# Moving parts of the scan's and of the deformable layer's elementwise work between VectorE, GpSimd and TensorE

## The chip, the cores and the metric

The kernel runs on one core of one Trainium2 chip. The metric is the time of one execution on the device, in microseconds (us); less is better. The engines are named as in the profile: PE is TensorE's matmul and PEld its weight load, DVE is VectorE, ACT is ScalarE, POOL is GpSimd, SP is SyncE, which issues most DMAs.

## The reference, cut to what matters

Four images of 128 channels and 128 x 128 positions, fp32, go through four layers, each `x = x + layer(group_norm(x))`.

- Layer 0 is a deformable 3 x 3 convolution. For each of the 9 taps and each position, a convolution gives an offset and a mask. The input is sampled at the offset place, bilinearly: `corner(y0, x0) + corner(y0, x0+1) + corner(y0+1, x0) + corner(y0+1, x0+1)`, each corner multiplied by its weight and the mask. Then the sampled values are multiplied by the tap's 128 x 128 weight.
- Layer 1 is a dilated convolution, layer 3 a 3 x 3 convolution with a difference term.
- Layer 2 has a selective scan: 128 channels, 16 states, four directions of 16,384 steps, for each image:

```
delta = softplus(dts + dt_b)
dA = exp(delta * A)                      # one per channel and state
h = h * dA + (delta * u) * b             # per channel and state; b per state
y = sum over the states of h * c
```

Before and after the scan stand projections, small convolutions, norms and a gate.

## The kernel before, in words

**Scan.** The positions of one image and direction are cut into 32 blocks of 512 (N); over four images and four directions that is `seq`, 512 blocks. A block has four groups g (NG = 4). A group holds 32 channels times four of their states on the 128 partitions, and has four tiles of 512 along the free axis, called states below (ng = 0 to 3); so 16 scans of 128 x 512 make up a block. For one group the engines do the following:

- SP spreads `delta` and `du = delta * u` from DRAM over the partitions (`spread`, L872); `bb` and `cb`, the b and c of the reference, are spread once for a block (L885).
- ACT copies `du` into a PSUM bank (`inputs_up`, L879). The bank carries the tag `dub`, of which there is one; `prepare` uses the same one for two projections.
- DVE forms the input of all four states in one product of 128 x 2048, `h = du * bb` (L972).
- ACT forms the decays, `exp(delta * A)`, in PSUM (`decay`, L899).
- DVE runs four scans in place (L1018). ACT copies the last column to `carry` (`carry_on`, L933).
- The product `h * cb` is done on two states at a time (`outputs`, L939, 128 x 1024), half 0 and half 1 of a group. It is POOL's. Beside the deformable layer half 1 is DVE's (`on_vector`). Beside layers that load PE, POOL also adds the last two states of each second group (L941), so that PE has one matmul less.
- PE sums over states and partitions with the matrix `gather` into `yacc` (`sums`, L913).

The tiles `h` have five buffers. `prepare(t + 2)` makes delta, du, b and c two blocks ahead. It is a generator: each `next(more, None)` in the scan's loop runs it up to its next `yield`, one slot at a time, 15 in a block. Softplus is `relu(v) + ln(1 + e) + (e - ((1 + e) - 1))` with `e = exp(-|v|)`: ACT computes the functions, POOL the two sums and the difference (L858, L860, L862), and then `du` (L864).

**Deformable layer.** For every block of 512 positions and tap (index n, 1152 in all, 288 for each image) `gather` reads, by four indirect DMAs from POOL's queue (L424), the four corners of each of 4 x 128 positions into the tile `g` of four buffers. ACT multiplies three corners by their weights (`weigh_low`, L438), the first into a PSUM bank `pw`. DVE adds the second and the third to it (`weigh`, L450, two instructions of 128 x 512) and then the fourth with its weight (L453, four of 128 x 128, into `v`). PE transposes `v` (`turn`, L461), ACT copies it out (`copy`, L465), PE multiplies by the tap's weights (`project`, L471). `weave` interleaves these steps: each has a delay in iterations, and stands in one of five places of an iteration. The delays are 0 for gather, 2 for weighing, 3 for turn and copy, 4 for project.

**Order.** The work on every engine is in program order (`keep_order`). The scan of image b runs beside the other layers of its neighbours: `together` lets a generator of the other layers advance with the scan's progress. `loads` writes into `beside["busy"]` which engine the layer at hand loads most: "POOL" beside the deformable layer, "PE" beside layers 1, 2 and 3 of most images, None otherwise. The first image's layers 0 and 1 have no scan to run beside. The order does not depend on any time, so the same instructions stand beside each other in every execution.

Of the kernel before, what the change touches and what calls it, by code (L numbers as in the profile page):

```python
# [10 lines left out]
F32 = mybir.dt.float32  # L11
# [3 lines left out]
ALU = mybir.AluOpType  # L15
# [3 lines left out]
P = 128  # L19
# [4 lines left out]
N = R * W  # L24
# [7 lines left out]
NG = 4  # L32
# [79 lines left out]
def conv_preact_kernel(ctx: ExitStack, tc: tile.TileContext, a: dict, nb: int):  # L112
    nc = tc.nc
    x_in, out = a["x"], a["out"]

    const = ctx.enter_context(tc.tile_pool(name="const", bufs=1))
    small = ctx.enter_context(tc.tile_pool(name="small", bufs=2))
    dram = ctx.enter_context(tc.tile_pool(name="dram", bufs=2, space=DRAM))
    pss = ctx.enter_context(tc.tile_pool(name="scps", bufs=1, space=PSUM))
# [11 lines left out]
    beside = {}  # L131
# [19 lines left out]

    ident = const.tile([P, P], F32, name="ident")
    make_identity(nc, ident)
    started = len(tc.nc.cur_bb.bb.instructions)
    nc.scalar.preload_act_table_set(LOG_EXP)
    gmat = load(const, a["gmat"], [P, P], "gmat_sb")
# [23 lines left out]
    with ExitStack() as s:  # L180
# [3 lines left out]
        for k in range(NDIR):  # L184
            pw = bank(0, "pwd")
# [112 lines left out]
    def layer0(st):  # L298
# [5 lines left out]
        with ExitStack() as s:  # L304
# [139 lines left out]

            def weigh(n):
                i, k, j, q = where(n)
                wv, g = got["i", j][0], got.pop(("g", n))
                pw = got.pop(("w", n)).rearrange("p (r c) -> p r c", r=R)
                for c in (1, 2):
                    nc.vector.tensor_add(pw, pw, g[:, :, c, :])  # L450
                got["v", n] = v = gp.tile([P, R, P], F32, name="v", bufs=2)
                for r in range(R):
                    nc.vector.scalar_tensor_tensor(  # L453
                        v[:, r, :], g[:, r, 3, :], wv[:, r, q, k, 3:4], pw[:, r, :], ALU.mult, ALU.add
                    )

            def turn(n):
                v = got.pop(("v", n))
                got["t", n] = pst = bank(1, "pst")
                for r in range(R):  # L460
                    nc.tensor.transpose(pst[:, r * P : (r + 1) * P], v[:, r, :], ident)  # L461

            def copy(n):
                got["c", n] = smp = pp.tile([P, N], F32, name="smp")
# [322 lines left out]
    def scan(pull):  # L787
# [14 lines left out]
        def decays(at):  # L802

            beside["decays"] = lambda: decays(at + 1)
            while ahead["made"] < min(at + 2, len(seq) * NST):
                decay(ahead["made"])
                ahead["made"] += 1
# [11 lines left out]
                    flush()  # L819
                blocks[t]["u"] = load(sp, blk(us[k % 2], i), [P, N], "u", bufs=2)  # L820

        def prepare(t):

            st, k, i, back = seq[t]
            c = blocks[t]
            if (st["b"], k) not in carries:
                carries[st["b"], k] = carry = small.tile([P, NST], F32, name="carry")
                nc.vector.memset(carry, 0.0)
            c["carry"] = carries[st["b"], k]
            u = c["u"]  # L830
            pdt = pss.tile([P, N], F32, name="pdt", tag="dub")
            nc.tensor.matmul(pdt, wd[:, k, :], u, start=True, stop=True)  # L832
            yield

            dtb = col(V_DTB + k)
            e = sp.tile([P, N], F32, name="e", bufs=1)
            nc.scalar.activation(e, pdt, AF.Abs, bias=dtb)  # L837
            steps = sp.tile([P, 2, N], F32, name="steps")
            delta, du = steps[:, 0, :], steps[:, 1, :]
            nc.scalar.activation(delta, pdt, AF.Relu, bias=dtb)  # L840
            yield
            nc.scalar.activation(e, e, AF.Exp, scale=-1.0)
            yield
            one_e = sp.tile([P, N], F32, name="one_e", bufs=1)
            nc.scalar.activation(one_e, e, AF.Identity, bias=1.0)
            yield
            px = pss.tile([P, N], F32, name="pxbc", tag="dub")
            nc.tensor.matmul(px, xbc[:, k, :], u, start=True, stop=True)  # L848
            ln = sp.tile([P, N], F32, name="ln", bufs=1)
            nc.scalar.activation(ln, one_e, AF.Ln)  # L850
            yield
            nc.scalar.activation(one_e, one_e, AF.Identity, bias=minus)  # L852
            bc = sp.tile([2 * NST, N], F32, name="bc")
            nc.scalar.copy(bc, px[0 : 2 * NST])  # L854
            c["bc"] = bcd = dram.tile([2, NST, N], F32, name="bcd", bufs=4)
            store(bcd.rearrange("j s t -> (j s) t"), bc)
            yield
            nc.gpsimd.tensor_sub(e, e, one_e)  # L858
            yield
            nc.gpsimd.tensor_add(ln, ln, e)  # L860
            yield
            nc.gpsimd.tensor_add(delta, delta, ln)  # L862
            yield
            nc.gpsimd.tensor_mul(du, delta, u)  # L864
            c["steps"] = sd = dram.tile([P, 2 * N], F32, name="stepsd", bufs=4)
            store(sd, steps.rearrange("p j t -> p (j t)"))
# [9 lines left out]
        def inputs_up(t, g):  # L876

            blocks[t]["pdu", g] = p = pss.tile([P, N], F32, name="dub", tag="dub")
            nc.scalar.copy(p, blocks[t]["p", g][:, 1, :])  # L879

        def spread_states(t, what):

# [52 lines left out]
        def outputs(t, g, half, engine=nc.gpsimd):  # L935

            c = blocks[t]
            h = c["h", g][:, 2 * half : 2 * half + 2, :]
            engine.tensor_mul(h, h, c["cb"][:, 2 * half : 2 * half + 2, :])  # L939
            if half and g % 2 and beside.get("busy") == "PE":  # L940
                engine.tensor_add(h[:, 0, :], h[:, 0, :], h[:, 1, :])  # L941
                c["added", g] = True
# [17 lines left out]
        for t, (st, k, i, back) in enumerate(seq):  # L960
            c = blocks[t]
            carry = c["carry"]
            more = prepare(t + 2) if t + 2 < len(seq) else iter(())
            if t > 0:
                fetch(t + 3)
            for g in range(NG):
                then = (t, g + 1) if g + 1 < NG else (t + 1, 0)
                soon = (t, g + 2) if g + 2 < NG else (t + 1, g + 2 - NG)
                before = (t, g - 1) if g else (t - 1, NG - 1)
                earlier = (t, g - 2) if g > 1 else (t - 1, g + NG - 2)  # L970
                c["h", g] = h = hp.tile([P, NG, N], F32, name="h")
                nc.vector.tensor_tensor(  # L972
                    h, c["pdu", g].unsqueeze(1).to_broadcast([P, NG, N]), c["bb"], ALU.mult
                )
                on_vector = beside.get("busy") == "POOL"
                if before[0] >= 0:
                    carry_on(*before, 1)
                if soon[0] < len(seq):
                    spread_steps(*soon)
                at = t * NST + g * NG  # L980
                decays(at)
                if g == 1:
                    if t + 1 < len(seq):
                        spread_states(t + 1, "bb")
                if g == 2 and t + 1 < len(seq):
                    spread_states(t + 1, "cb")
                if g == 3 and back:
                    c["before"] = load(sp, blk(st["y"][k % 2], i), [P, N], "before", bufs=1)
                for ng in range(NG):
                    n = g * NG + ng  # L990
                    if ng == 1:
                        decays(at + 1)
                        if before[0] >= 0 and not on_vector:
                            outputs(*before, 1)
                        if g > 1 and then[0] < len(seq):
                            inputs_up(*then)
                        if earlier[0] >= 0:
                            sums(*earlier, 1)
                    if ng == 2 and g == 1 and t > 0:
                        finish(t - 1)  # L1000
                    if n % NST and ng != 2:
                        next(more, None)
                    if ng == 2 and before[0] >= 0 and on_vector:
                        outputs(*before, 1, nc.vector)
                    if ng == 2:
                        carry_on(t, g, 0)
                        decays(at + 2)
                        next(more, None)
                        if g < 2:
                            inputs_up(*then)  # L1010
                    if ng == 3:
                        outputs(t, g, 0)
                        if before[0] >= 0:
                            sums(*before, 0)
                    o, f = h[:, ng, :], c["a", n]
                    if back:
                        o, f = o[:, ::-1], f[:, ::-1]
                    nc.vector.tensor_tensor_scan(o, f, o, carry[:, n : n + 1], ALU.mult, ALU.add)  # L1018
                    if ng == 3:
                        decays(at + 3)  # L1020
                    yield (t * NST + n + 1) / slots
            for _ in more:
                pass
# [409 lines left out]
```

## Time and profile before

| | us |
|---|---|
| median of three runs | 22,396.11 (22,355.13 to 22,411.09) |
| the profiled execution's own time | 21,942.39 |
| its span, first to last instruction | 21,940.6 |
| PE, PEld busy | 16,289.2 (74%), 6635.1 (30%) |
| DVE busy | 18,903.6 (86%) |
| ACT busy | 16,411.9 (75%) |
| POOL busy | 17,213.1 (78%) |
| mean granted TensorE clock | 0.874 |

Busy time says how long an engine had an instruction under way; its share of the span is an average over stages that have different limits. A row of the groups of instructions has the line, engine and operation, the names out<-in, shapes and count, then the busy time and the mean in ns, and then the engine's idle time before these instructions with what ended it. A fp32 matmul appears as two records, a transpose as one.

### The profile page before, as it was taken

Reading aid. Unit: us, or ns where it says so; the run is one execution under the profiler, and the core shown is the slowest. Engines: PE = TensorE matmul, PEld = TensorE weight load, DVE = VectorE, ACT = ScalarE, POOL = GpSimd, SP = SyncE. Lnnn points to the kernel's source line nnn. Section 1 sums busy time; section 2 is a strip of 40 time slices with the busy share of each in tenths; the row PEclk is TensorE's granted clock in tenths of the full one; section 3 lists DMA queues with packets and bytes.
Section 4 is the critical chain, followed back from the end, with each engine's and each line's share of the span. In section 5 each row is a group of like instructions: output and inputs, shape, how many; then the busy total and the mean of one; then the engine's idle time right before and its main releaser. Section 6 shows DMA issues by size and latency. Waiting matters only on the chain. (4 is left out here: it accounts for less than half of the span.)

```text
span 21940.6 us, 177438 instructions
## 1 busy us (share of the span) xinstructions
PE 16289.2 (74%) x37000; PEld 6635.1 (30%) x37000; DVE 18903.6 (86%) x19821; ACT 16411.9 (75%) x37350; POOL 17213.1 (78%) x11496
## 2 busy tenths in 40 slices
PE   4557866666788878666688888766687878778788
PEld 1223322222333333222233333322233323233333
DVE  4554899999998899899998899998998899999994
ACT  5885868888688766788868776688877877666673
POOL 4773878877888888778788888787878889877884
PEclk6668988888999989888899999887898999999999
DMA  8775687777766968777776787777776677555674
GB/s 250 229 226 178 210 287 243 243 237 237 235 215 216 256 224 272 233 250 249 241 231 220 221 254 249 245 246 245 246 256 210 219 217 233 194 195 202 208 233 132
DMA packets 2578828, 5038.92 MB, mean 230 GB/s; under 512 B 1060736, under 2 KB 1333576, under 8 KB 2435408
## 3 DMA queue, kind: packets, MB, share of 16 engines
q1 hardware_dynamic: 2209104, 3819.31, 53.3%
q0 software_dynamic: 368640, 1208.25, 18.1%
q14 instruction: 782, 6.41, 0.1%
q8 instruction: 302, 4.95, 0.1%
HBM read 4082.03 MB, written 874.52 MB: 226 GB/s over the span
## 5 line engine op out<-in xcount | busy, mean ns | idle before, releaser
L1018 DVE TENSOR_TENSOR_SCAN h<-pa,carry,h 128x512 f32<-128x512 f32 x8192 | 9998.0, 1267 | 495.7 <-ACT pa L899 283.6
L913 PE MATMUL yacc<-h,gather_sb 128*128 128x512 f32 x15264 | 8338.4, 676 | 1770.5 <-POOL h L939 1170.3
L939 POOL TENSOR_TENSOR h<-h,cb 128x1024 f32<-128x1024 f32 x3740 | 8787.1, 2363 | 1093.0 <-ACT carry L933 1076.8
L424 POOL DMA_INDIRECT g<-table,idx x4608 | 4552.7, 988 | 1616.0 <-issue 1059.3
L899 ACT ACTIVATE pa<-spread,neg_a 128x512 f32<-128x512 f32 x8192 | 5488.2, 682 | 271.7 <-DVE h L1018 270.8
L972 DVE TENSOR_TENSOR h<-dub,bb 128x2048 f32<-128x2048 f32 x2048 | 4659.9, 2275 | 418.9 <-ACT dub L879 162.9
L913 PEld LDWEIGHTS yacc<-h,gather_sb 128*128 128x128 f32 x15264 | 3133.5, 216 | 6082.3 <-issue 3392.2
L461 PE MATMUL pst<-ident,v 128*128 128x128 f32 x4608 | 1194.5, 371 | 2578.5 <-DVE v L453 2236.1
L438 ACT ACTIVATE g<-g,wt 128x128 f32<-128x128 f32 x9216 | 2877.5, 389 | 301.5 <-DMA g<-table,idx 298.5
L933 ACT COPY carry<-h 128x2 f32<-128x2 f32 x4096 | 769.0, 188 | 3035.9 <-DVE h L1018 3031.8
L450 DVE TENSOR_TENSOR pw<-pw,g 128x512 f32<-128x512 f32 x2304 | 1597.7, 693 | 1073.6 <-ACT pw L438 1022.6
L438 ACT ACTIVATE pw<-g,wt 128x128 f32<-128x128 f32 x4608 | 1693.6, 368 | 291.2 <-DVE v L453 177.4
L461 PEld LDWEIGHTS pst<-ident,v 128*128 128x128 f32 x4608 | 718.5, 158 | 3938.6 <-issue 1901.5
L858 POOL TENSOR_TENSOR e<-e,one_e 128x512 f32<-128x512 f32 x512 | 651.2, 1272 | 1294.8 <-ACT one_e L852 1258.2
L471 PE MATMUL acc<-smp,w_sb 128*128 128x512 f32 x2304 | 1550.9, 762 | 56.1 <-DVE x L478 52.8
L879 ACT COPY dub<-spread 128x512 f32<-128x512 f32 x2048 | 1198.7, 585 | 391.2 <-DVE h L972 212.7
L453 DVE SCALAR_TENSOR_TENSOR v<-g,wt,pw 128x128 f32<-128x128 f32 x4608 | 1292.8, 342 | 113.7 <-DVE pw L450 2.8
L1238 PE MATMUL p<-xn,w_l_sb 128*128 128x508 f32 (+2 forms) x2304 | 1132.9, 610 | 1.8 <-ACT xn L1217 1.8
L848 PE MATMUL pxbc<-u,xbc_sb 128*128 128x512 f32 x1024 | 590.5, 660 | 394.4 <-DVE h L972 385.9
L721 PE MATMUL px<-win,convw_sb 128*128 128x508 f32 (+1 forms) x1536 | 786.8, 610 | 36.1 <-DMA win<-win 34.8
L941 POOL TENSOR_TENSOR h<-h 128x512 f32<-128x512 f32 x558 | 710.8, 1274 | 43.7
L832 PE MATMUL pdt<-u,wd 128*128 128x512 f32 x1024 | 562.4, 632 | 193.3 <-DVE h L972 127.4
(170 smaller groups left out, 16751.3 us busy)
## 6 DMA issues: line engine op xcount, KB each, us to landing
spread<-stepsd SPq DMA_DIRECT2D x2048, 512.0 KB, 4.3
bb<-bcd SPq DMA_DIRECT2D x512, 1024.0 KB, 8.0
cb<-bcd SPq DMA_DIRECT2D x512, 1024.0 KB, 9.1
stepsd<-steps SPq DMA_DIRECT2D x512, 512.0 KB, 3.5
table<-gt SPq DMA_DIRECT2D x512, 256.0 KB, 4.8
g<-table,idx POOLq DMA_INDIRECT x4608, 3.8
u<-urow SPq DMA_DIRECT2D x256, 256.0 KB, 3.5
yrow<-y SPq DMA_DIRECT2D x256, 256.0 KB, 9.3
```

The source lines that it names most:

```text
L424: nc.gpsimd.indirect_dma_start(out=g[:, r].rearrange("p q c -> p (q c)"), out_offset=None, in_=table, in_offset=bass.IndirectOffsetOnAxis( ...
L438: nc.scalar.activation(pw[:, r * P : (r + 1) * P] if c == 0 else g[:, r, c, :], g[:, r, c, :], AF.Copy, scale=wv[:, r, q, k, c : c + 1],)
L450: nc.vector.tensor_add(pw, pw, g[:, :, c, :])
L453: nc.vector.scalar_tensor_tensor(v[:, r, :], g[:, r, 3, :], wv[:, r, q, k, 3:4], pw[:, r, :], ALU.mult, ALU.add)
L461: nc.tensor.transpose(pst[:, r * P : (r + 1) * P], v[:, r, :], ident)
L471: nc.tensor.matmul(got["a", i], w0[:, k, :], got.pop(("c", n)), start=k == 0, stop=k == KK - 1)
L879: nc.scalar.copy(p, blocks[t]["p", g][:, 1, :])
L899: nc.scalar.activation(pa, blocks[t]["p", g][:, 0, :], AF.Exp, scale=neg_a[:, k, n : n + 1])
L913: nc.tensor.matmul(c["y"], gather[:, g, :], c["h", g][:, ng, :], start=g == 0 and ng == 0, stop=last and ng == parts[-1] and not second,)
L939: engine.tensor_mul(h, h, c["cb"][:, 2 * half : 2 * half + 2, :])
L972: nc.vector.tensor_tensor(h, c["pdu", g].unsqueeze(1).to_broadcast([P, NG, N]), c["bb"], ALU.mult)
L1018: nc.vector.tensor_tensor_scan(o, f, o, carry[:, n : n + 1], ALU.mult, ALU.add)
```

## The change

- A constant `less`, the negative of the identity matrix, is made at the start.
- **Fourth neighbour.** `weigh` no longer adds the third corner (index 2, already weighted by ACT). `turn` instead adds it on PE: for each of the four rows, one matmul of `g[:, r, 2, :]` with the identity and one of `v[:, r, :]` with the identity accumulate into the same part of the bank. They take the place of one transpose. The tile `g` is released after `turn`, not after `weigh`.
- **Softplus's sums.** If the block starts beside the deformable layer (`on_pe`), `prepare` skips two slots, sums `e`, minus `one_e`, `ln` and `delta` by four matmuls into the bank `dub`, and copies the sum to `delta` on ACT one slot later. `du` follows in slot 11 where it was slot 10. `inputs_up` for groups 2 and 3 then stands at ng = 2, where that for groups 0 and 1 already is.
- **Half 0 of the last group.** Beside the deformable layer, half 0 of group 3 goes to DVE as well.
- **Fourth state's input.** Where the deformable layer is not beside the scan, POOL forms the input of the last state of every second group (`last_input`, called at ng = 2 of groups 1 and 3 for the group after), straight from `spread`. DVE's product L972 then covers three states.

```diff
@@ constants
     make_identity(nc, ident)
+    less = const.tile([P, P], F32, name="less")
+    nc.vector.tensor_scalar_mul(less, ident, -1.0)
@@ weigh(n)
-                wv, g = got["i", j][0], got.pop(("g", n))
+                wv, g = got["i", j][0], got["g", n]
                 pw = got.pop(("w", n)).rearrange("p (r c) -> p r c", r=R)
-                for c in (1, 2):
-                    nc.vector.tensor_add(pw, pw, g[:, :, c, :])
+                nc.vector.tensor_add(pw, pw, g[:, :, 1, :])
@@ turn(n)
-                v = got.pop(("v", n))
+                v, g = got.pop(("v", n)), got.pop(("g", n))
                 got["t", n] = pst = bank(1, "pst")
                 for r in range(R):
-                    nc.tensor.transpose(pst[:, r * P : (r + 1) * P], v[:, r, :], ident)
+                    dst = pst[:, r * P : (r + 1) * P]
+                    nc.tensor.matmul(dst, g[:, r, 2, :], ident, start=True, stop=False)
+                    nc.tensor.matmul(dst, v[:, r, :], ident, start=False, stop=True)
@@ prepare(t, on_pe=False)
-            nc.gpsimd.tensor_sub(e, e, one_e)
-            yield
-            nc.gpsimd.tensor_add(ln, ln, e)
-            yield
-            nc.gpsimd.tensor_add(delta, delta, ln)
-            yield
+            if on_pe:
+                yield
+                yield
+                pd = pss.tile([P, N], F32, name="psum", tag="dub")
+                for n, (t, sign) in enumerate(((e, ident), (one_e, less), (ln, ident), (delta, ident))):
+                    nc.tensor.matmul(pd, sign, t, start=n == 0, stop=n == 3)
+                yield
+                nc.scalar.copy(delta, pd)
+                yield
+            else:
+                nc.gpsimd.tensor_sub(e, e, one_e)
+                yield
+                nc.gpsimd.tensor_add(ln, ln, e)
+                yield
+                nc.gpsimd.tensor_add(delta, delta, ln)
+                yield
             nc.gpsimd.tensor_mul(du, delta, u)
@@ new function
+        def last_input(t, g):
+            c = blocks[t]
+            c["h", g] = h = hp.tile([P, NG, N], F32, name="h")
+            nc.gpsimd.tensor_mul(h[:, NG - 1, :], c["p", g][:, 1, :], c["bb"][:, NG - 1, :])
@@ the scan's loop
-            more = prepare(t + 2) if t + 2 < len(seq) else iter(())
+            on_pe = beside.get("busy") == "POOL"
+            more = prepare(t + 2, on_pe) if t + 2 < len(seq) else iter(())
...
-                c["h", g] = h = hp.tile([P, NG, N], F32, name="h")
+                ready = ("h", g) in c
+                if not ready:
+                    c["h", g] = hp.tile([P, NG, N], F32, name="h")
+                h, n = c["h", g], NG - 1 if ready else NG
                 nc.vector.tensor_tensor(
-                    h, c["pdu", g].unsqueeze(1).to_broadcast([P, NG, N]), c["bb"], ALU.mult
+                    h[:, 0:n, :], c["pdu", g].unsqueeze(1).to_broadcast([P, n, N]), c["bb"][:, 0:n, :], ALU.mult
                 )
...
-                        if g > 1 and then[0] < len(seq):
+                        if g > 1 and then[0] < len(seq) and not on_pe:
                             inputs_up(*then)
...
+                        if g % 2 and not on_vector and then[0] < len(seq):
+                            last_input(*then)
                         next(more, None)
-                        if g < 2:
+                        if (g < 2 or on_pe) and then[0] < len(seq):
                             inputs_up(*then)
                     if ng == 3:
-                        outputs(t, g, 0)
+                        outputs(t, g, 0, nc.vector if on_vector and g == NG - 1 else nc.gpsimd)
```

More of the change, by code (lines that the diff above doesn't have):

```diff
@@ L820, in fetch, with prepare @@
                 blocks[t]["u"] = load(sp, blk(us[k % 2], i), [P, N], "u", bufs=2)
-        def prepare(t):
+        def prepare(t, on_pe=False):
             st, k, i, back = seq[t]
```

## The prediction

> **What bounds the kernel now.** I read the busy time by stretch first, because the page's averages mix stages: 0 to 1650 us is the first image's deformable layer alone; three stretches (3250-5350, 8850-10850, 14120-16080, together 6060 us) are the scan beside the next image's deformable layer ("deformable stage" below); the other 13,400 us or so, from 2000 on, are the scan beside other layers ("scan stages"). Columns: stretch, its length, then busy us (and instructions) of PE, PEld, DVE, ACT, POOL, the granted clock of TensorE, DMA share, GB/s.
>
> ```profile
> 9000.00:10500.00 1500.00, 988.45 (x2577) 409.52 (x2578) 1361.49 (x2119) 1328.29 (x3687) 1203.42 (x1067) 0.81 0.77 247
> 6000.00:8500.00 2500.00, 2016.89 (x4285) 820.27 (x4284) 2293.59 (x1724) 1860.16 (x3567) 2134.86 (x1180) 0.93 0.73 233
> 19000.00:20500.00 1500.00, 1182.96 (x2556) 482.92 (x2555) 1449.04 (x1048) 925.55 (x1858) 1200.16 (x611) 0.95 0.57 197
> 500.00:1500.00 1000.00, 578.57 (x1580) 217.93 (x1580) 580.46 (x1418) 864.86 (x2606) 756.78 (x799) 0.67 0.76 228
> 18000.00:18500.00 500.00, 409.70 (x825) 160.12 (x824) 471.49 (x343) 387.39 (x763) 464.90 (x262) 0.95 0.77 237
> ```
>
> In the scan stages DVE is the bound: 97% at 19000, 92% at 6000. POOL follows at 80 and 85%, and at 18000 (four POOL products per block of the output stage) it has 93%.
>
> The deformable stage seems to have three near-equal engines: DVE 91%, ACT 89%, POOL 80%. The groups of lines of 9000 to 10500 (busy, mean ns, then idle before and its releasers) settle it:
>
> ```profile
> L424 POOL DMA_INDIRECT g<-table,idx x899 | 892.4, 993 | 269.4 <-issue 216.7 <-ACT pw L438 21.1 <-DMA g<-table,idx 5.0
> ...
> L450 DVE TENSOR_TENSOR pw<-pw,g 128x512 f32<-128x512 f32 x450 | 311.4, 692 | 103.4 <-ACT pw L438 95.1 <-DMA g<-table,idx 0.4
> ...
> L461 PE MATMUL pst<-ident,v 128*128 128x128 f32 x900 | 223.1, 359 | 500.7 <-DVE v L453 420.2 <-ACT g L438 28.5 <-ACT smp L465 19.5
> L939 POOL TENSOR_TENSOR h<-h,cb 128x1024 f32<-128x1024 f32 x84 | 199.4, 2374 | 9.1 <-ACT carry L933 8.2
> ```
>
> The 269 us before the gathers are mostly "issue", some 0.3 us between one gather and the next. With them POOL is at 1203 + 269 + about 25 = 1497 of 1500 us: POOL is the bound here, at 1.25 us a gather. The lone stage confirms it: 400 gathers in 500 us, 1.25 each, four per neighbour point, 5.0 us a point.
>
> **What the Trainium skill says.** "Perfetto Trace Analysis", Transposes, advises a real transpose for a logical one, not a standard matmul. The change does the opposite. The trace shows the price: a transpose is one record, an fp32 matmul two (15,264 yacc records for 7632 matmuls). Starts from the timeline:
>
> ```profile
> 9203.73 0.60 PE L374 MATMUL ptp<-ident,pos_c 128*128 128x128 f32 x4
> 9204.17 1.02 PE L471 MATMUL acc<-smp,w_sb 128*128 128x512 f32 x2
> 9205.03 0.60 PE L461 MATMUL pst<-ident,v 128*128 128x128 f32 x4
> ```
>
> Four transposes take 9204.17 - 9203.73 = 0.44 us, 0.11 each; two 512-wide records 0.86, 0.43 each (granted clock 0.96 from 9203 to 9206; "full clock" below).
>
> ```profile
> 7240.25 0.64 PE L1055 MATMUL pe<-cmat_sb,event_sb 128*128 128x128 f32 x2
> 7240.67 2.77 PE L913 MATMUL yacc<-h,gather_sb 128*128 128x512 f32 x3
> ```
>
> A 128-wide matmul proper takes two records in 0.42 us, in a stretch where TensorE has half its clock (0.50 from 7239 to 7243), so 0.21 at full clock, an estimate; I use 0.11 a record, as for a transpose. "TensorE: Matmul & The Clock Gate", Part 1, says the array is held to half clock until it has been busy for some microseconds. The trace agrees in direction: granted 0.67 with PE 58% busy, 0.81 at 66%, 0.95 at 79%. "GPSIMD Engine Reference", Specifications, says POOL shares its SBUF interfaces with DVE instructions that have two SBUF inputs. Of the moved work only the product on DVE (L939, h and cb both in SBUF) is such. The views here bear it out only mildly (the last softplus product, L864, means 1555 ns in this stage, 1277 at 19000).
>
> **The change part by part.**
>
> *Fourth neighbour.* One of two adds (L450, 692 ns) goes from every point: 1152 x 0.69 = 797 us of DVE. 288 are in the lone stage, where gathers set 5.0 us a point: worth nothing. In 9000-10500, 225 points, it frees 156 us of DVE. PE gets, per point, eight matmuls (16 records) for four transposes: 1.76 us for 0.44 at full clock, +1.32. Their turn is now also the last reader of the gather buffer g (four buffers), instead of DVE's v. The gather that reuses it is emitted one iteration later, so this is hidden unless PE lags; then POOL waits, with products and softplus queued behind it.
>
> *Softplus on PE.* Three POOL sums leave (1283 + 1276 + 1277 = 3.84 us per scan block). PE gets four matmuls, 8 x 0.43 = 3.4 us, ACT one PSUM copy at 0.58 (as L465, 576 ns). That copy waits for PE; behind it on ACT stand inputs_up and the next decays, for which DVE's scans wait. The copy comes one scan slot (4.5 us) after the matmuls, so I allow 1 us a block, bounds 0 and 3. The inputs_up of groups 2 and 3 moves one slot later, where groups 0 and 1 have it already without a DVE wait: nothing. The product for du and the store of steps on SP move one slot later too (11 of 15), and are read half a block after: nothing.
>
> *Half of the last group to DVE.* POOL loses 2.37 us a block, DVE gets 1.27.
>
> Sum for 9000-10500 (21 blocks): POOL 1497 - 21 x 6.2 = 1367; ACT 1328 + 12 = 1340; DVE 1361 - 156 + 27 = 1232; PE at full clock, records times spacing: before 1222 x 0.43 + 924 x 0.11, and the position matmuls, four abreast, 426/4 x 0.43 = 46: 673 us in all; after, 673 + 297 + 72 = 1042. So POOL gives up to 6.2 us a block, but ACT stands 27 us behind it at 1340, and with that queue in order two full engines do not interlock perfectly. I take 3.5 of 6.2 us: 21 blocks then take 1426 us, POOL 96%, ACT 94%, DVE 86%, PE 73% at full clock. Blocks in the stage: 356 products on DVE / 4 = 89. **89 x 3.5 = 310 us**; bounds -100 and 500.
>
> *Fourth state on POOL.* In the other 512 - 89 = 423 blocks two groups each, 846, have 1536 elements on DVE in place of 2048. From L972 (2275 ns) and L450 (692 at 512) the slope is 1.03 ns an element, so 0.53 us: 846 x 0.53 = 450 us at most. POOL gets 846 x 1.27 (L858's shape) = 1075 us. Ahead of the scan that needs it lie five others and one product, over 8 us, and spread and bb have landed: the product is early enough. It stands in POOL's queue before outputs(t, g, 0), whose sums PE awaits with a group of slack. At 19000, 51 blocks: DVE 1449 - 54, POOL 1200 + 130 = 1330 of about 1446: full gain. At 6000, 77 blocks: POOL 2135 + 196 = 2331 of 2418, 96%: part of it. At 18000 POOL would need 465 + 41 = 506 of 500: a loss. Window by window (full gain unless POOL passes 98%) I get about 330 us, and take 80% of it for interlocking. **270 us**; bounds 0 and 400.
>
> The making of the negative identity and the rest of the start: one small DVE instruction under loads, nothing.
>
> Sum: -580 of the profiled execution's 21,942.39 us (span 21,940.6, 1.8 around it). That execution is 2.07% under the median of the runs, 22,396.11; nothing I read explains this, so I scale: (21,942 - 580) x 1.0207 = 21,800 us.
>
> **Rivals.** (a) *PE becomes the bound in the deformable stage.* 1042 us of full-clock work need a clock of 1042/1426 = 0.73 to fit; below that the turns are late and hold the gather buffers, and POOL stops for them. For: it has 0.81 there now, and 0.67 in the lone stage, with waits on v between. Against: more matmuls mean fewer idle stretches, and stretches with PE near 80% show 0.95. The scan gain is eaten, with 0.3% more, at 336/89 = 3.8 us a block more than now, a stretch of 1580 us, clock 0.66. At 0.60: 1737 us, +11.3 a block, +1000 - 270 = +730, time 23,145. (b) *POOL is the new bound in the scan stages*: what DVE saves comes back as waits on products; only 310 stays: 22,080. For: 93% at 18000 and nothing spare there. Against: at 19000 POOL waits 159 us for carry and 139 for softplus's input, room for 130. (c) *ACT holds the deformable stage* by waiting for PE's sums and transposes: only 270 stays: 22,120. (d) *Both*: nothing moves. (e) That the edits don't act is excluded by counts: 846 and 1152 follow from loops already counted in the trace.
>
> **Numbers.** Forecast with both gains 0.60; (b) 0.13, (c) 0.10, both faster; (d) 0.06; (a) 0.11. About 0.3% is what a measurement can tell from no change: faster 0.83, same 0.06, slower 0.11. Low end: 500 + 400 gained, 21,480; the high end takes in (b), (c) and most of their lesser forms, 22,320.
>
> **What would show it.** Right: L450 with 1152 records; L972 with 846 forms of 1536 at about 1.75 us; L424's idle time in the deformable stage no longer the same "issue" with POOL full, blocks of 68 us rather than 71; granted clock there above 0.85; DVE still over 94% at 19000 and blocks of 28.4 us rather than 29.4. Wrong: gathers waiting for PE pst; ACT's copy of delta waiting more than 3 us a block; scans waiting for POOL h.

## Result and the profile after

| | median us | range us |
|---|---|---|
| before | 22,391.8 | 22,355.13 to 22,411.09 (4 runs) |
| after | 22,050.5 | 22,042.83 to 22,073.78 (4 runs) |
| after / before | 0.9851 | 95% interval 0.9834 to 0.9868 |

The change saves 341 us. The prediction had 596 (22,396 to 21,800); its range holds the result.

One thing is needed to read the numbers: the runs fell on several chips, and the same kernel takes 21,921 to 21,930 us on two of them (called *first kind* below) and 22,390 to 22,412 us on two others (*second kind*), so a time is compared only with that of before on the same chip. Each of these chips was measured at one time only, so that the chip and not the moment makes the kind is likely, not shown. By their times, the profiled execution of before (21,942) came from the first kind, and the runs in the table and the profile after from the second. So stages are compared here between two traces from one chip of the first kind, before once more (span 21,923.3 us) and after once more (span 21,550.3 us). The change is worth 0.9829 [0.9813, 0.9846] there.

The stretches of that trace of after, which answer to the five shown of before (columns as there: stretch, length, busy us and instructions of PE, PEld, DVE, ACT, POOL, then granted clock, DMA share, GB/s):

```profile
9000.00:10500.00 1500.00, 1246.13 (x5594) 763.35 (x5593) 1248.88 (x1948) 1374.75 (x3826) 1103.17 (x1013) 0.93 0.78 255
6000.00:8500.00 2500.00, 2068.69 (x4404) 849.69 (x4405) 2250.51 (x1752) 1875.98 (x3598) 2353.02 (x1348) 0.92 0.75 239
19000.00:20500.00 1500.00, 1212.95 (x2637) 496.44 (x2636) 1442.99 (x1082) 965.65 (x1946) 1374.72 (x743) 0.96 0.63 211
500.00:1500.00 1000.00, 759.01 (x3968) 509.14 (x3969) 441.76 (x1218) 866.46 (x2604) 756.21 (x799) 0.90 0.76 228
18000.00:18500.00 500.00, 396.71 (x786) 153.25 (x785) 435.38 (x330) 369.46 (x727) 484.01 (x284) 0.93 0.69 217
```

The load has moved as the diff says. Beside the deformable layer (9000) DVE fell from 1361 to 1249 us, POOL from 1203 to 1103, and PE rose from 988 to 1246 at a clock of 0.93 where it had 0.81. In the scan stages POOL rose to 92 to 97%, and at 18000 DVE is no longer full: 87%, where it had 94%.

Cut into stages by the same gathers and scans in both traces (us, first kind):

| stage | before | after | difference | predicted |
|---|---|---|---|---|
| lone deformable stage | 1440.6 | 1441.9 | +1 | 0 |
| rest of the start | 569.1 | 578.2 | +9 | 0 |
| deformable layer beside the scan | 5894.3 | 5699.8 | -194 | -310 |
| scan stages | 13,682.4 | 13,494.2 | -188 | -270 |
| end | 336.8 | 336.3 | 0 | 0 |

On the first kind the gain lies in the two places where it was predicted, at 63 and 70% of its size. Two more traces of before on this kind have 13,694 and 13,705 us for the scan stages and 5887 us for the deformable layer beside the scan, so a difference between two traces can be off by some 10 to 20 us.

On the second kind the lone stage is slower: the profile after (same kernel, same instructions) shows

```profile
500.00:1500.00 1000.00, 674.28 (x3269) 484.10 (x3269) 367.79 (x1017) 705.85 (x2144) 622.00 (x656) 0.81 0.64 187
```

That is 656 gathers in 1000 us where the first kind has 799. The lone stage takes 1754.1 us there instead of 1441.9. Beside the trace of before that I had for the prediction, this looked like damage done by the change. It was the first thing to test.

### The profile page after: what moved, and what is told of

It is laid out like the page before. It is cut to its first block, busy times and chain, and to the rows that moved or that the text cites. A ratio compares the mean times of both kernels' runs of the same rounds, so it can differ in the third digit from the quotient of the medians.

```text
span 22046.9 us, 206313 instructions
## 1 busy us (share of the span) xinstructions
PE 17530.0 (80%) x51536; PEld 8506.2 (39%) x51536; DVE 17759.7 (81%) x18759; ACT 16420.1 (74%) x37439; POOL 17657.2 (80%) x11985
## 5 line engine op out<-in xcount | busy, mean ns | idle before, releaser
L933 PE MATMUL yacc<-h,gather_sb 128*128 128x512 f32 x15264 | 7958.5, 648 | 1906.5 <-POOL h L959 1303.9
L996 DVE TENSOR_TENSOR h<-dub,bb 128x2048 f32<-128x2048 f32 (+1 forms) x2048 | 4210.4, 2056 | 519.8 <-ACT dub L893 517.4
L464 PE MATMUL pst<-ident,g 128*128 128x128 f32 x9216 | 2134.8, 319 | 1327.6 <-ACT smp L469 1097.8
L464 PEld LDWEIGHTS pst<-ident,g 128*128 128x128 f32 x9216 | 1686.8, 224 | 2174.2 <-ACT smp L469 1614.3
L465 PE MATMUL pst<-ident,v 128*128 128x128 f32 x9216 | 2129.5, 318 | 321.9 <-DVE v L454 170.8
L451 DVE TENSOR_TENSOR pw<-pw,g 128x512 f32<-128x512 f32 x1152 | 797.0, 692 | 1961.2 <-ACT pw L440 1555.4
L465 PEld LDWEIGHTS pst<-ident,v 128*128 128x128 f32 x9216 | 1674.8, 227 | 419.2 <-DVE v L454 225.0
L475 PE MATMUL acc<-smp,w_sb 128*128 128x512 f32 x2304 | 1287.6, 642 | 21.4 <-DVE x L482 14.8
L469 ACT COPY smp<-pst 128x512 f32<-128x512 f32 x1152 | 668.1, 580 | 776.3 <-remote 578.2
L899 POOL TENSOR_TENSOR h<-spread,bb 128x512 f32<-128x512 f32 x845 | 1079.5, 1278 | 15.9 <-DMA spread<-stepsd 10.2
```

The costliest lines, as they stand in the source:

```text
L464: nc.tensor.matmul(dst, g[:, r, 2, :], ident, start=True, stop=False)
L465: nc.tensor.matmul(dst, v[:, r, :], ident, start=False, stop=True)
L933: nc.tensor.matmul(c["y"], gather[:, g, :], c["h", g][:, ng, :], start=g == 0 and ng == 0, stop=last and ng == parts[-1] and not second,)
L996: nc.vector.tensor_tensor(h[:, 0:n, :], c["pdu", g].unsqueeze(1).to_broadcast([P, n, N]), c["bb"][:, 0:n, :], ALU.mult)
```

## Experiments

The expectations name theories by letters. **A**: eight matmuls in place of four transposes lengthen the loop of the lone stage. **B**: the neighbour on PE is what the deformable stage beside the scan gains from. **C**: the slow lone stage belongs to the chip, not to the change. Where they say "place", they mean what is called a kind of chip here, and GpSimd is POOL. They cut the stages slightly otherwise, so their sums differ by a few us. The kernels below are "after" with parts taken back. Those of the first group ran on one chip of the first kind, with before at 21,921.46 us.

**Before, unchanged.**

> The kernel before, unchanged, for its stages in the same session as the rest. Its first profiled execution took 21,942 us, its runs 22,355 to 22,411. If the 450 us between them lie in one stage, a second profile shows that stage longer: the lone deformable stage (5.0 us a point, 1442 us from first to last gather) is the suspect, because there every point is one short loop through POOL, ACT, DVE and PE; it would then take about 1890 us, 6.6 us a point. If they are spread over all stages, every stage is 2% longer, and the lone one takes about 1470 us.

Measured: 21,921.45 us, ratio 0.9998 [0.9989, 1.0007]; lone stage 1439.9 us. The chip is not the one of the first comparison, and before is 470 us faster on it, so this run says nothing of the slow one. The lone stage that was suspected is the place: in before's form it takes 1843 to 1867 us on the second kind (runs below), where 1890 was expected.

**After without the neighbour on PE.** `less`, softplus on PE, half 0 on DVE and `last_input` stay.

```diff
-                nc.vector.tensor_add(pw, pw, g[:, :, 1, :])
+                for c in (1, 2):
+                    nc.vector.tensor_add(pw, pw, g[:, :, c, :])
...
-                    nc.tensor.matmul(dst, g[:, r, 2, :], ident, start=True, stop=False)
-                    nc.tensor.matmul(dst, v[:, r, :], ident, start=False, stop=True)
+                    nc.tensor.transpose(pst[:, r * P : (r + 1) * P], v[:, r, :], ident)
```

> The changed kernel with the fourth neighbour added on DVE and a transpose again, everywhere. Theory A (the neighbour on PE costs the lone stage, where v, turn, copy and the gather buffer form a loop): the lone stage goes back from 6.1 us a point to 5.0, 1754 to about 1440 us, so 310 us less there; beside the scan DVE gets 156 us of each 1500 back and the stage is 0 to 150 us longer in all; net 22,050 - 310 + 75 = 21,800. Theory B (the neighbour on PE is what brings the gain): slower than the changed kernel by 100 to 300 us, 22,150 to 22,350.

Measured: 21,856.27 us, ratio 0.9970 [0.9958, 0.9983]. The times expected were those of the second kind; by what they say of the difference, B holds: the run is 306 us slower than after on the first kind (21,550.6 us, below), and A's shorter lone stage isn't there to be won (1440.4 us). The scan stages have their gain (13,495.9 us), but the deformable stage takes 6009.3 us, longer than before's 5894.3. POOL has lost 6.2 us a block here, just as in the prediction. What it does with the time is seen in the stretch 9000 to 10500 and its groups (busy, mean ns, then the idle time before them and what ended it):

```profile
9000.00:10500.00 1500.00, 1017.83 (x2691) 424.57 (x2690) 1347.45 (x2079) 1304.53 (x3610) 1044.11 (x958) 0.82 0.74 241
```

```profile
L426 POOL DMA_INDIRECT g<-table,idx x876 | 871.3, 995 | 363.4 <-issue 223.9 <-ACT pw L440 107.6 <-ACT g L440 10.6
...
L452 DVE TENSOR_TENSOR pw<-pw,g 128x512 f32<-128x512 f32 x438 | 303.3, 693 | 113.8 <-ACT pw L440 105.1 <-DMA g<-table,idx 0.9
...
L464 PE MATMUL pst<-ident,v 128*128 128x128 f32 x876 | 213.7, 353 | 467.5 <-DVE v L455 397.5 <-ACT g L440 31.3 <-ACT smp L468 18.5
```

POOL is 159 us less busy than before, yet makes fewer gathers, 876 instead of 899. It waits for ACT's products instead: 107.6 us, where before had 21.1. DVE and ACT are not full either (90 and 87%). So POOL's load does not set the pace here; POOL keeps pace with a loop that runs through ACT and DVE. What made that loop longer isn't separated. DVE has one more product a block (half 0, 103 where it would be 82 in this stretch, 1.32 us each), over 89 blocks 117 us; measured is 6009.3 - 5889.2 = 120 us against the kernel with `last_input` alone, below. But ACT now also waits for softplus's sums on PE:

```profile
ACT steps L868 <- PE psum L866: 37.9, 9, 5.4
```

That is 37.9 us in 20.5 blocks, 1.8 us a block, which could cost as much. The run took work off POOL and put some on DVE, ACT and PE at once; POOL's share alone was not taken away with the neighbour on DVE.

**After with the neighbour on PE only beside the scan.** In the lone stage DVE adds it and PE transposes.

```diff
+                on_pe = got["pe", n] = beside.get("busy") == "POOL"
...
+                for c in (1,) if on_pe else (1, 2):
+                    nc.vector.tensor_add(pw, pw, g[:, :, c, :])
...
+                    if on_pe:
                         nc.tensor.matmul(dst, g[:, r, 2, :], ident, start=True, stop=False)
                         nc.tensor.matmul(dst, v[:, r, :], ident, start=False, stop=True)
+                    else:
+                        nc.tensor.transpose(dst, v[:, r, :], ident)
```

> The changed kernel with the fourth neighbour on PE only beside the scan; in the lone stage two adds on DVE and a transpose as before. Theory A: the lone stage takes about 1440 us again and the rest is as in the changed kernel: 22,050 - 310 = 21,740. Theory B: the lone stage is at its 6.1 us a point for another reason (the chip of the session, gathers), and the time stays at 22,050 within 60.

(Its theory B is C of the list above.) Measured: 21,547.98 us, ratio 0.9831 [0.9815, 0.9848]; deformable stage 5704.9, lone stage 1440.8 us. The chip is of the first kind, so neither expected time applies and A is still open. Against the kernel above, the neighbour on PE is worth 304 us beside the scan, 3.4 us a block, with POOL already 6.2 us a block lighter. The 864 points of the stage took 864 x 0.69 = 596 us of adds from DVE, 6.7 us a block, and half of that shows in the time. A rival is TensorE's clock, 0.93 in 9000 to 10500 where the kernel above has 0.82: a faster PE could shorten the loop too. But the waits of ACT, DVE and POOL for PE in that stretch add up to 121 us here and 67 us in the kernel above, so PE holds the others more with the neighbour on it, not less. The lighter DVE is the likeliest cause left; no run took work off DVE alone.

**Before with `last_input` alone.** Built from the kernel without the neighbour on PE:

```diff
-            on_pe = beside.get("busy") == "POOL"
+            on_pe = False
...
-                        outputs(t, g, 0, nc.vector if on_vector and g == NG - 1 else nc.gpsimd)
+                        outputs(t, g, 0)
```

> The kernel before with the fourth state's input on GpSimd alone. By stage, the two profiles put the gain of the scan stages at 216 us; the prediction had 270. If the parts add up, 22,390 - 216 = 22,175 (0.990). If the gain of the scan stages needs the other parts, nothing is left: 22,390.

Measured: 21,727.96 us, ratio 0.9911 [0.9894, 0.9928], near the 0.990 expected if the parts add up. Scan stages 13,494.1, deformable stage 5889.2 us. Every kernel with `last_input` has the scan stages at 13,477 to 13,499 us, whatever else it has. The part in the scan stages doesn't depend on the rest of the change.

**After and before on a third chip.** The second group of runs (below) had fallen on a chip of the second kind, so both kernels ran once more, to have after where A and C differ.

> The changed kernel a third time. So far two places were seen: one where the kernel before takes 21,921 us and its lone deformable stage 1440, one where it takes 22,390 and the lone stage, in the form of before, about 1850. On the second place the changed kernel takes 22,048 (0.985), lone stage 1755. If this run falls on the first place: theory A (matmuls for transposes lengthen the loop of the lone stage) says 1640 to 1755 us there and a total of 21,750 to 21,860; theory C (the lone stage is bound by the gathers at 1.25 us each, the rest hides) says 1440 and a total of 21,550, 0.983. If it falls on the second: 22,048 again.

> The kernel before, for a profile beside the run above. On the first place it is known (lone stage 1440, the three deformable stages 2045, 1913 and 1925 us). On the second, the sum of what is known leaves a lone stage of about 1850 and deformable stages of 5920 in all, scan stages within 10 us of those of the first place.

Measured: after 21,550.6 us, ratio 0.9829 [0.9813, 0.9846], lone stage 1441.9; before 21,925.1 us in its one run, lone stage 1440.6. With all its matmuls, after has the lone stage of before. **A is refuted** for this kind, and C holds as far as it goes: the slow lone stage comes with the kind of chip. The gathers of the lone stage (500 to 1500), here, and after that in the run of after on the second kind:

```profile
L426 POOL DMA_INDIRECT g<-table,idx x799 | 757.1, 948 | 244.0 <-issue 133.8 <-ACT pw L440 41.7 <-DMA g<-table,idx 22.5
```

```profile
L426 POOL DMA_INDIRECT g<-table,idx x656 | 620.4, 946 | 381.7 <-ACT smp L469 195.4 <-issue 161.9 <-PE pst L465 18.7
```

One gather is busy equally long, 0.95 us. Only the waits differ.

**After again, and its two small parts on the deformable stage.** All four ran on one chip of the second kind, with before at 22,390.15 us. The last three are built from the kernel with the neighbour on PE only beside the scan, so that their lone stage is that of before. Their expectations were written for the first kind, so only the differences between these runs say something.

> The changed kernel, unchanged, measured beside the kernel before where that takes 21,921 us and not 22,391. Theory A (the lone stage is slower by 315 us with the neighbour on PE, wherever it runs): 21,548 + 315 = 21,860, ratio 0.997. Theory C (the slow lone stage of the first profile belongs to the place of that run, which also made the kernel before 2% slower): the lone stage takes about 1440 us, the time is that of the kernel with the neighbour on PE only beside the scan, 21,550 within 40, ratio 0.983 as in the first comparison.

No edit: this is after as it stands. Measured: 22,047.58 us, ratio 0.9851 [0.9835, 0.9867]. Deformable stage 5895.5, lone stage 1755.5 us.

Without softplus on PE and without half 0 on DVE (only the scan's loop is edited, as for `last_input` alone):

```diff
-            on_pe = beside.get("busy") == "POOL"
+            on_pe = False
...
-                        outputs(t, g, 0, nc.vector if on_vector and g == NG - 1 else nc.gpsimd)
+                        outputs(t, g, 0)
```

> Two parts only: the neighbour on PE beside the scan, and the fourth state's input. Softplus's sums and half 0 of the last group stay on GpSimd. By the prediction GpSimd is the bound beside the scan, so this gets nothing there: 21,728, as with the input alone. By the rival that came up (DVE is the bound, since relieving GpSimd by 6.2 us a block without the neighbour lost 128 us), the neighbour brings most of the gain: 21,550 to 21,620.

Measured: 22,161.13 us, ratio 0.9905 [0.9889, 0.9922]. Deformable stage 5914.3, lone stage 1842.8 us.

With softplus on PE, half 0 of group 3 on POOL:

```diff
-                        outputs(t, g, 0, nc.vector if on_vector and g == NG - 1 else nc.gpsimd)
+                        outputs(t, g, 0)
```

> As the kernel with the neighbour on PE only beside the scan (21,548), but half 0 of the last group stays on GpSimd: DVE has 1.27 us a block less, GpSimd 2.37 more. If GpSimd is near its bound: slower by up to 89 x 2 = 180. If DVE or ACT is: faster by up to 89 x 1.2 = 107, or equal.

Measured: 22,156.77 us, ratio 0.9897 [0.9880, 0.9913]. Deformable stage 5915.3, lone stage 1858.6 us.

With half 0 on DVE, softplus on POOL:

```diff
-            on_pe = beside.get("busy") == "POOL"
+            on_pe = False
```

> As the kernel with the neighbour on PE only beside the scan (21,548), but softplus's three sums stay on GpSimd: GpSimd has 3.84 us a block more, ACT 0.58 less, PE 3.4 less, and ACT's wait for PE is gone. If GpSimd is near its bound: slower by up to 89 x 3.5 = 310. If ACT is: faster by 50 or more.

Measured: 22,224.85 us, ratio 0.9924 [0.9907, 0.9941]. Deformable stage 5970.4, lone stage 1858.0 us.

The 6.2 us a block that the two edits take from POOL, 550 us over 89 blocks, move the stage by 19 us, and by 11 us against the second run of that kernel below, no more than two traces of one kernel can differ. Softplus alone moves nothing, and half 0 alone costs 56 us. So POOL's load doesn't set the pace with the neighbour on PE either, on this kind of chip. Whether it does on the first kind, where the stage takes 5700 us and not 5896, was not run. Why half 0 costs something alone and nothing together with softplus isn't settled by these runs.

The lone stage is 87 us shorter in after than in the kernel without softplus and half 0. Neither of those edits acts there, so it is the neighbour on PE. On this kind of chip the lone stage is not set by the gathers' pace. Whether the DVE add that went shortens it, or TensorE's clock (0.81 in 500 to 1500 where that kernel has 0.64), isn't separated.

**Less work for ACT.** With the neighbour on PE, ACT is the fullest engine of the deformable stage. Here, at every third point beside the scan, ACT's first product is left out, and DVE weighs that corner in one pass with the add of the second.

```diff
+                    if c == 0 and beside.get("busy") == "POOL" and n % 3 == 0:
+                        return
...
+                    pw = v
+                    for r in range(R):
+                        nc.vector.scalar_tensor_tensor(
+                            v[:, r, :], g[:, r, 0, :], wv[:, r, q, k, 0:1], g[:, r, 1, :], ALU.mult, ALU.add
+                        )
```

> The changed kernel, and beside the scan, in every third point, DVE weighs the first corner and adds the second in one pass (four scalar_tensor_tensor of 128 x 128, 1.37 us, for one add of 0.69), so that ACT's four products into the bank (1.56 us) go. On the first place ACT is busy 1375 of 1500 us in the deformable stage, DVE 1249: after this about 1258 and 1300 for the same work. If ACT is what bounds the stage now: 5700 us of deformable stages shorten by 2 to 4%, 100 to 200 us; 21,550 becomes 21,350 to 21,450 (ratio 0.974 to 0.979; on the second place 0.976 to 0.981). If the loop v, turn, copy with its single banks bounds it: no change beyond 40 us. If DVE does again: slower by up to 100.

Measured, on another chip of the second kind (before 22,411.62 us): 22,043.1 us, ratio 0.9838 [0.9821, 0.9854]; after had 0.9851 [0.9835, 0.9867], so no difference is shown. The load did move, as the stretch 9400 to 10400 shows for this kernel, and below it for after:

```profile
9400.00:10400.00 1000.00, 807.77 (x3576) 498.14 (x3575) 840.65 (x1392) 808.84 (x2236) 720.74 (x648) 0.91 0.75 245
```

```profile
9400.00:10400.00 1000.00, 819.79 (x3613) 498.55 (x3611) 797.68 (x1258) 883.45 (x2457) 710.30 (x650) 0.92 0.76 246
```

ACT lost 75 us and DVE got 43, and the gathers stay at 594 in both stretches. The whole deformable stage went from 5895.5 to 5878.3 us. Taking that much from ACT at DVE's cost changes nothing, so ACT's load alone doesn't set the pace either.

**Neighbour and `last_input` once more**, the kernel without softplus and half 0, meant for a chip of the first kind:

> The neighbour on PE beside the scan and the fourth state's input alone, again: softplus's sums and half 0 stay on GpSimd. On the second place this had 5911 us in the deformable stages, the changed kernel 5893. On the first the changed kernel has 5700, the kernel before 5893. If GpSimd is the bound there, as the prediction says, these two parts leave it at about 5890 and the total at 21,730. If the neighbour's relief of DVE is the gain: 5700 to 5760, total 21,550 to 21,610.

Measured: 22,188.13 us, ratio 0.9904 [0.9887, 0.9920], deformable stage 5906.2 us. It fell on the second kind again and repeats 0.9905. What the two small edits are worth on the first kind stays open.

## Why the prediction was right, and where it was not

**Direction and counts** were right, and on the first kind the place too. The groups of after for the whole execution (first kind) have the counts that the prediction gave (845 for 846):

```profile
L996 DVE TENSOR_TENSOR h<-dub,bb 128x2048 f32<-128x2048 f32 (+1 forms) x2048 | 4212.8, 2057 | 520.6 <-ACT dub L893 517.5
...
L451 DVE TENSOR_TENSOR pw<-pw,g 128x512 f32<-128x512 f32 x1152 | 796.5, 691 | 1546.9 <-ACT pw L440 1530.6
...
L899 POOL TENSOR_TENSOR h<-spread,bb 128x512 f32<-128x512 f32 x845 | 1077.3, 1275 | 20.0 <-DMA spread<-stepsd 13.9
```

**The prices** held. The turn on PE, starts in the timeline:

```profile
9402.15 0.38 PE L464 MATMUL pst<-ident,g 128*128 128x128 f32 x2
9402.37 0.39 PE L465 MATMUL pst<-ident,v 128*128 128x128 f32 x2
...
9403.93 1.02 PE L475 MATMUL acc<-smp,w_sb 128*128 128x512 f32 x2
```

From 9402.15 to 9403.93 are 1.78 us for eight matmuls; priced at 1.76. ACT's copy of delta waited 31.8 us for its 22 blocks in 9000 to 10500, 1.4 us a block; priced at 1.

**The deformable stage: the step that failed is "POOL is the bound here, at 1.25 us a gather".** It rested on 1497 of 1500 us being busy, "issue" or waited for, and on "issue" being a fixed cost of a gather. The sum was right and the conclusion wrong. With the neighbour left on DVE, the edits that take 6.2 us a block from POOL made the stage 120 us longer, though by the prediction's own sums every engine stayed more than 100 us below the 1497. The neighbour's move to PE, to which the forecast gave no part of the gain, brought 304 us, measured on top of the lighter POOL; whether it needs the lighter POOL on the first kind stays open. The gain is the net of these two, by the two traces of before and after 194 us, or 2.2 us a block, where I had 3.5. The error in the mechanism is larger than in the number. In after, gathers do wait for others, as the prediction listed for "right", but for another reason, and one sign listed for "wrong", gathers waiting for PE pst, is there too (32.7 us in the first line below; 9000 to 10500, first kind):

```profile
L426 POOL DMA_INDIRECT g<-table,idx x926 | 920.7, 994 | 354.0 <-issue 197.2 <-ACT pw L440 53.5 <-PE pst L465 32.7
...
L464 PE MATMUL pst<-ident,g 128*128 128x128 f32 x1852 | 399.9, 301 | 147.5 <-ACT smp L469 147.5
...
L451 DVE TENSOR_TENSOR pw<-pw,g 128x512 f32<-128x512 f32 x231 | 159.1, 689 | 208.7 <-ACT pw L440 205.6 <-DMA g<-table,idx 2.1
```

Here "issue" is 197.2 us for 926 gathers, 0.21 each, where before had 216.7 for 899, 0.24; it was not fixed. No engine is full: ACT has 92%, and PE (83%), DVE (83%) and POOL (74%) each wait for another. PE waits for ACT's copy out of the one bank `pst`, and DVE for ACT's product in the bank `pw`. What the runs show is that neither POOL's load (the run without softplus and half 0) nor ACT's (the run with a third of its first products left out, which also gave DVE more) sets the pace by itself, both on the second kind, and that the neighbour's move from DVE to PE shortens the stage on the first. That the hand-over through the banks is what remains is my reading; more banks were not tried. A block takes 1500 / (87/4) = 69.0 us (87 products of L996 in the stretch), where 68 was predicted.

**The scan stages: the term that was mis-sized is the share kept, "80% of it for interlocking".** I had 330 us and took 270; measured are 188 in this pair of traces (200 and 211 with the two other traces of before), 42% of the 450 at most. Where the full gain was predicted, most of it came, as the groups of 19000 to 20500 show:

```profile
L996 DVE TENSOR_TENSOR h<-dub,bb 128x2048 f32<-128x2048 f32 x105 | 239.3, 2279 | 16.9 <-ACT dub L893 16.9
L996 DVE TENSOR_TENSOR h<-dub,bb 128x1536 f32<-128x1536 f32 x105 | 183.0, 1743 | 9.6 <-ACT dub L893 9.6
```

The two shapes are 0.536 us apart (priced at 0.53). 210 products are 52.5 blocks of 28.6 us, where before had 204 and 29.4 us; 28.4 was predicted, so 0.8 of 1.0 us. DVE is at 96%. Elsewhere the saving came back as waits. The waits of DVE from 16200 to 21000, first of before, then of after (us in total, times, longest):

```profile
DVE h L1018 <- ACT pa L899: 78.4, 77, 18.0
DVE h L972 <- issue: 49.7, 109, 7.7
DVE h L972 <- ACT dub L879: 43.4, 72, 3.3
DVE h L972 <- POOL h L939: 37.4, 90, 2.1
```

```profile
DVE h L996 <- ACT dub L893: 197.2, 290, 8.2
DVE h L1044 <- ACT pa L919: 121.3, 110, 18.4
```

The shorter product meets ACT's copy into the single bank `dub`, which isn't there yet, and the scans meet decays that aren't. Over the whole execution the kernel with `last_input` alone has 451 us less of products on DVE, and 126 us more idle time before them and 92 more before the scans. I had looked only at POOL as the engine that could eat the gain. At 18000 it does have 97%, as the prediction said; but what DVE waits for there is ACT too. POOL may still stand behind it. From 16200 to 21000, first of before, then of after:

```profile
PE yacc L913 <- POOL h L939: 522.7, 324, 5.0
ACT e L837 <- PE pdt L832: 31.4, 17, 7.3
```

```profile
PE yacc L933 <- POOL h L959: 662.4, 378, 5.0
ACT e L841 <- PE pdt L836: 100.8, 57, 7.8
```

PE's sums wait longer for POOL's products, and ACT, whose work is in order, waits longer for the projection that PE makes after such sums. No run separates this path from the single bank.

**The scaling.** "Nothing I read explains this, so I scale": the 2.07% between the profiled execution and the median was, by the times above, a difference between chips. It sits mostly in the lone stage, not spread over the kernel as the factor had it. Before's form of the lone stage takes 1843 to 1867 us on the second kind and 1441 on the first, so some 400 to 430 of the 470 us between the two times of before. The scan stages are alike, 13,477 to 13,499 and 13,486 to 13,496 us in the kernels with `last_input`. On the second kind the change gets some 90 to 110 us from the lone stage and keeps the 188 or so of the scan stages, if before's scan stages are alike there too. That leaves 341 - 100 - 188, about 50 us, for the deformable stage, an estimate, since no trace of before was taken there. So on the kind of chip on which the 341 us were measured, some 100 come from a stage to which the prediction gave nothing, and the deformable stage gives about a sixth of its 310. That the total still fell inside the range is in part luck.

**The rivals.** (a) PE as the bound: its clock did not fall but rose to 0.93 (0.91 on the second kind), far above the 0.73 that PE's work needs. "TensorE: Matmul & The Clock Gate", Part 1, in the Trainium skill ties the clock to how busy the array has been recently; here it went from 0.81 at 66% busy to 0.93 at 83%, which agrees. (b) POOL full in the scan stages: in part, 92 to 97%, though DVE's direct waits for its products (37.4 us from 16200 to 21000 in before) are gone. (c) ACT holding the deformable stage by its transfers: nearer to what is seen than the forecast's own reason, but not by its load. (d) no effect: excluded, the interval ends at 0.9868.

## What to carry to other kernels

An engine whose busy, issue and wait times add up to the span can be following a loop as well as leading it; take work off it alone before building a forecast on it. Here 6.2 us a block less for POOL gained nothing, with 1.3 us a block more for DVE, while the engine that was fullest by busy time alone, DVE at 91%, was the one whose relief went with the gain of 304 us. Work moved off a full engine is worth its full time only until the next hand-over is late, so list every producer of that engine's operands (here ACT's copy into a bank of which there is one), not only the engine that gets the work. When a profile and the runs differ by more than the runs among themselves, find the stage that differs before scaling.

## What was unexpected of the hardware

The same kernel takes 21,921 to 21,930 us on two chips and 22,390 to 22,412 on two others, steadily within 0.3% on each. In after, POOL's, ACT's and DVE's instructions of the lone stage are equally long on both: a gather 948 and 946 ns, ACT's products 390 ns, DVE's add 700 ns. PE's are longer on the second kind, 348 against 311 ns for the first of the turn's matmuls, at a granted clock of 0.81 against 0.90; whether that is a cause or follows from PE being less busy (67 against 76%) isn't shown. For the other engines what differs is when the next instruction starts. The waits of that stage (500 to 1500 us) in after on the second kind:

```profile
ACT smp L469 <- remote: 268.2, 79, 6.5
POOL g L426 <- ACT smp L469: 195.4, 78, 3.3
```

ACT waits 268 us before its copy for something the trace doesn't name, and POOL waits for that copy. On the first kind the copy is preceded by 2.8 us of idle time in all, and POOL's gathers wait 1.5 us for it. What is late, PE's result or the signal of it, and why on these chips, is not settled.
